# The first image's preparation reordered: its load on two queues, the weights' sums behind its parameters, four evictions moved to VectorE

## The chip, the cores and the metric

The kernel runs on one core of one Trainium2 chip. The metric is the device time of one execution in microseconds (us). Engines are named as in the profile: PE (TensorE; PEld is its weight load), DVE (VectorE), ACT (ScalarE), POOL (GpSimd) and SP (SyncE, which here only issues DMAs). ScalarE issues DMAs too; in the profile SP's DMA queue is q1 and ScalarE's is q10, and the issues themselves appear as SPq and ACTq.

## What is computed

The input x is 8 images of 256 channels, 56 by 56, fp32. Layer 0 is an involution on the group-normalised input: two 1x1 convolutions make a 7x7 kernel for each pixel and each of 16 channel groups, and this kernel weights the pixel's neighbourhood. Layer 1 is two 3x3 convolutions with ternary weights, each with a batch norm. Both layers add their input.

```python
def _L0_conv_ref(x, w_reduce, b_reduce, w_span, b_span):
    ker = jnp.einsum('bchw,oc->bohw', x, w_reduce) + b_reduce[None, :, None, None]
    ker = jnp.einsum('bchw,oc->bohw', ker, w_span) + b_span[None, :, None, None]
    ker = ker.reshape(B, G, 1, K * K, H, W)
    ...
    out = (ker * patches).sum(axis=3)
    return out.reshape(B, C, H, W)
...
# --- layer 0 (conv_preact) ---
x = x + _L0_conv_ref(_gn(x), L0_conv_w_reduce, ...)
# --- layer 1 (conv_preact) ---
x = x + _L1_conv_ref(_gn(x), L1_conv_w1, ...)
```

`_gn` normalises each image in 32 groups of 8 channels, without a scale or shift of its own. `_L1_conv_ref` quantizes each weight tensor to -1, 0, 1 by thresholds from its mean, maximum and minimum, and adds the centre tap once more.

## The kernel before, in words

The first phase is the involution. An image is cut into four quarters of 64 channels (`NCQ` = 4); a quarter's tile `x` holds 128 partitions (64 channels by two half images) of 1568 elements, and is loaded by `load_x` in two DMAs of 392 KB. Ahead of the loop over quarters and rows stands a preparation, and only there does the change edit anything. Each engine works through its own instructions in the order in which the program text issues them (a scheduler keeps that order here, and a helper `pin` fixes it inside the loop). The preparation runs as follows.

- **Loads.** ScalarE's queue issues five constants through `loaded` (L114: grp_sb, and g1, b1, g2, b2 of the two batch norms). SP's queue issues the eight pieces of the first image (L610). ScalarE then issues the constants made by `fixed` (L677: rims_sb, ident_sb, half_sb), br and wr in two pieces each (L693, L694), wl (L695) and bt (L696). SP issues the first 3x3 weights into `wf` in two pieces (L703), the span weights and their biases for the sums (L942, L943), and the first five neighbourhood tiles q (L728), two of which use the buffers of those two loads again.
- **Statistics.** VectorE takes bn_stats over each piece of x (L149) and aggregates them for each quarter (L620).
- **Sums.** VectorE sums the span weights over the 49 taps into `wsum` and `bsum` (L945) and spreads `wsum` into `wsx` (L946). `wsx` is the weight of the matmuls `ks` (L786), and `bsum` goes into `shift` (gn1b, L638), a bias of the same step; both are read at the end of the quarter's preparation.
- **Parameters.** `params(0)` averages the statistics over groups by a matmul with grp_sb (L156), copies the means out of PSUM (gm, L160), does a second matmul for the variance (L168), adds epsilon (ve, L135), takes the square root on ScalarE (L137), and refines its reciprocal on VectorE. It scales the reducing weights wr into `wrn` (L629), makes the scales `gn1s` (L636), `shift` (L638), and, through the matmuls br (L644), the bias `brn` (L647). The matmuls rim (L651) carry the means to the padding.
- **Reduction.** The first 1x1 convolution, matmuls pk (L713), is evicted by ScalarE into `kr` with the bias brn (L722). In between, a generator `extremes` searches wf: VectorE takes maximum and minimum of six pieces (L224, L225), ScalarE sums each piece (L227), and small matmuls (L255, L256, L265) combine them across partitions.
- **Generation.** `generate(0, 0, ...)` makes the per-pixel kernels of the first quarter: 14 units, each a pair of PSUM banks filled by matmuls pg (L820). Six banks are in rotation, so three units are in flight. ScalarE evicts the second bank (odd groups) with one activation for each position in the unit, and another for the last row's part where there is one (L824); VectorE evicts the first bank (even groups) with one or two additions (L828). The units take 3, 3 and 2 positions for each of two group pairs, and then 4 positions each. The matmuls ks and their activations (L794) end the quarter.

Then the loop over rows begins, with the matmuls pa (L852). In it the same generator works one quarter ahead. After the involution come the two 3x3 convolutions (matmuls L522) and a last elementwise pass. The compiled streams give each DMA one of eight completion semaphores in turn, in the order of the text, and a DMA's issue waits, on its own queue's engine, until the earlier DMA with the same semaphore has landed.

Of the kernel before, what the change touches and what calls it, by code (L numbers as in the profile page):

```python
# [11 lines left out]
ALU = mybir.AluOpType  # L12
AX = mybir.AxisListType
# [4 lines left out]
P = 128  # L18
# [3 lines left out]
K, PAD, G = 7, 3, 16  # L22
KK = K * K
# [5 lines left out]
CH = P // 2  # L29
NCQ = C // CH  # L30
GQ = G // NCQ
# [10 lines left out]
NQ = QY * QX  # L42
# [15 lines left out]
          32: (2, 0, 3), 33: (2, 3, 3), 34: (2, 6, 3)}  # L58
A_COLS = (NT * NP + NE * PX) * GQ

PER_ROW = (2, 2, 2, 1, 2, 2, 1, 2, 2, 0)
NQB = 5
PLEAD = 2
# [26 lines left out]
def involution_tri_block_kernel(  # L90
# [3 lines left out]
    nc = tc.nc  # L94
# [14 lines left out]
    def const_tile(shape, name):  # L109
        return const.tile(shape, F32, tag=name, name=name)  # L110

    def loaded(shape, name, src):
        t_ = const_tile(shape, name)
        nc.scalar.dma_start(t_, src)  # L114
        return t_

    grp_sb = loaded([P, P], "grp_sb", grp)
# [33 lines left out]
    def group_norm_params(mv, dst, psum_tile, name, means=None):  # L151


        n = mv.shape[1]
        ps = psum_tile(f"gnp_{name}")
        nc.tensor.matmul(ps[:, :2 * n], grp_sb, mv.rearrange("p n s -> p (n s)"),  # L156
                         start=True, stop=True)
        yield
        gm = small.tile([P, n, 2], F32, tag=f"gn_gm{n}", name=f"gm_{name}")
        nc.vector.tensor_copy(gm.rearrange("p n s -> p (n s)"), ps[:, :2 * n])  # L160
        if means is not None:
            means.append(gm)
        d = small.tile([P, n], F32, tag=f"gn_d{n}", name=f"d_{name}")
        nc.vector.tensor_tensor(d, mv[:, :, 0], gm[:, :, 0], ALU.subtract)
        nc.vector.tensor_tensor(d, d, d, ALU.mult)
        yield
        ps2 = psum_tile(f"gnp2_{name}")
        nc.tensor.matmul(ps2[:, :n], grp_sb, d, start=True, stop=True)  # L168
        yield
        var = small.tile([P, n], F32, tag=f"gn_var{n}", name=f"var_{name}")  # L170
        nc.vector.tensor_tensor(var, ps2[:, :n], gm[:, :, 1], ALU.add)
        rs = rstd_of(var, GN_EPS, name)
        nc.vector.tensor_copy(dst[:, :, 0], rs)
        nc.vector.scalar_tensor_tensor(dst[:, :, 1], gm[:, :, 0], -1.0, rs, ALU.mult, ALU.mult)
# [404 lines left out]
    with ExitStack() as ph1:  # L579
# [3 lines left out]
        def ps_bank(name):  # L583
            return ps_p.tile([P, 512], F32, tag="ps", name=name)

        def ps_pair(name):
            return [ps_bank(f"{name}_{i}") for i in range(2)]

        def ps_one(name):
            ps = row_ps[-1] if row_ps else ps_a.tile([P, 512], F32, tag="pa", name=name)  # L590
            return ps[:, TX * 2 * NP:]
# [10 lines left out]
        work = ph1.enter_context(tc.tile_pool(name="work", bufs=2))  # L602
        apool1 = ph1.enter_context(tc.tile_pool(name="apool1", bufs=1))

        def load_x(b, c, j):

            if j == 0:
                xs[b, c] = xpool.tile([P, NHW], F32, tag="x", name=f"x_{b}_{c}")
            part = slice(j * NHW // 2, (j + 1) * NHW // 2)
            nc.sync.dma_start(xs[b, c][:, part], x[b, c, :, part])  # L610

        def gn1_stats(b, c, j):

# [5 lines left out]
            if j == NCB - 1:  # L619
                nc.vector.bn_aggr(mvs[b][:, c, :], gst1[c].rearrange("p n s -> p (n s)"))  # L620

        def params(b):


            dst = small.tile([P, NCQ, 2], F32, tag="gn1", name=f"gn1_{b}")
            means = []
            yield from group_norm_params(mvs.pop(b), dst, ps_one, f"a{b}", means)
            for c in range(NCQ):
                nc.vector.tensor_scalar(  # L629
                    wrn[:, c, :].rearrange("p (i r) -> p i r", i=2),  # L630
                    wr[:, c, :].unsqueeze(1).to_broadcast([P, 2, CR]),
                    dst[:, c, 0:1], None, ALU.mult)

            scales = small.tile([P, NCQ, 2 + GQ], F32, tag="gn1s", name=f"gn1s_{b}")
            for c in range(NCQ):
                nc.vector.tensor_scalar(scales[:, c], half_sb, dst[:, c, 0:1], None, ALU.mult)  # L636
            shift = small.tile([P, NCQ], F32, tag="gn1b", name=f"gn1b_{b}")
            nc.vector.tensor_tensor(shift, dst[:, :, 1], bsum, ALU.mult)  # L638
            for _ in range(3):
                yield  # L640
            ps = ps_one(f"br_{b}")
            for c in range(NCQ):
                for i in range(2):
                    nc.tensor.matmul(ps[i * CR:(i + 1) * CR, :1], wr[:CH, c, :], dst[:CH, c, 1:2],  # L644
                                     start=(c == 0), stop=(c == NCQ - 1))
            yield
            nc.vector.tensor_tensor(brn, br, ps[:, :1], ALU.add)  # L647
            yield
            ps = ps_bank(f"rim_{b}")
            for c in range(NCQ):  # L650
                nc.tensor.matmul(ps[:NQ, c * P:(c + 1) * P],  # L651
                                 means[0][:, c, 0:1].to_broadcast([P, NQ]), ident_sb,
                                 start=True, stop=True)
            rim = small.tile([P, NCQ, P], F32, tag="rim", bufs=1, name=f"rim_{b}")
            nc.scalar.copy(rim[:NQ].rearrange("p c f -> p (c f)"), ps[:NQ, :NCQ * P])
            prm[b] = dst, scales, shift, rim
# [11 lines left out]
        gst1, mvs = {}, {}  # L668
        prm, xs = {}, {}
        for c in range(NCQ):  # L670
            for j in range(2):
                load_x(0, c, j)

        def fixed(shape, name, src=None, pool=fix):
            t_ = pool.tile(shape, F32, tag=name, name=name)
# [7 lines left out]
        bt = fixed([NQ, NCQ, GQ, NP], "bt", pool=early)  # L683

        wsum, wsx = fixed([P, G], "wsum"), fixed([P, NCQ, CH], "wsx")
        rims_sb = fixed([P, 5], "rims_sb", rims)
        bsum = fixed([P, NCQ], "bsum")
# [6 lines left out]
            nc.scalar.dma_start(wr[j * CH:(j + 1) * CH], w_red.rearrange("(t p) o -> p t o", p=CH))  # L694
        nc.scalar.dma_start(wl, w_line)  # L695
        nc.scalar.dma_start(bt, b_tile)  # L696


        nf = CT * 9 * C
# [100 lines left out]
                    nc.gpsimd.tensor_tensor(x_, x_, v, ALU.add)  # L800
                yield

        def generate(b, c, a):

            whole, rest = (v.rearrange("q t (g p) -> q g p t", g=GQ) for v in views(a))
            for u, (gp, p0, n) in enumerate(UNITS):
                ps = ps_pair(f"pg_{b}_{c}_{u}")
                nt = NT + (NE if p0 < PX else 0)  # L810
                g = 2 * gp
                parts = [(whole, 0, NT)] + ([(rest, NT, nt)] if NT < nt else [])

                for j in range(n):
                    py, px = (p0 + j) // PX, (p0 + j) % PX
                    o = py * QX + px
                    for i in range(2):
                        rows = slice(i * CR, (i + 1) * CR)
                        dst = ps[0][:NQ, j:n * nt:n] if i == 0 else ps[1][:NQ, j * nt:(j + 1) * nt]
                        nc.tensor.matmul(dst, wl[rows, c, gp, o:o + NQ], kr[py][rows, px, :],  # L820
                                         start=True, stop=True)
                for j in range(n):
                    for dst, t0, t1 in parts:
                        nc.scalar.activation(  # L824
                            dst[:, g + 1, p0 + j], ps[1][:NQ, j * nt + t0:j * nt + t1],
                            AF.Identity, bias=bt[:, c, g + 1, p0 + j:p0 + j + 1])
                for dst, t0, t1 in parts:
                    nc.vector.tensor_tensor(  # L828
                        dst[:, g, p0:p0 + n].rearrange("q p t -> q t p"),
                        ps[0][:NQ, t0 * n:t1 * n].rearrange("q (t p) -> q t p", p=n),  # L830
                        bt[:, c, g, p0:p0 + n].unsqueeze(1).to_broadcast([NQ, t1 - t0, n]), ALU.add)
                yield
            yield from constant(b, c)
# [37 lines left out]
        queue = [(b, c, ty) for b in range(B) for c in range(NCQ) for ty in range(TY)]  # L871
# [66 lines left out]
        for _ in range(2):  # L938
            held.append(qpool.tile([P, TX, P], F32, tag="q", name=f"sums{len(held)}"))
        wv, bv = (t_.rearrange("p k c -> p (k c)")[:, :n_ * KK]  # L940
                  for t_, n_ in zip(held, (G, NCQ)))
        nc.sync.dma_start(wv, w_all)  # L942
        nc.sync.dma_start(bv, b_all)  # L943
        for dst, v in ((wsum, wv), (bsum, bv)):
            nc.vector.tensor_reduce(dst, v.rearrange("p (g k) -> p g k", k=KK), AX.X, ALU.add)  # L945
        nc.vector.tensor_copy(wsx.rearrange("p c (g i) -> p (c g) i", g=GQ),  # L946
                              wsum.unsqueeze(2).to_broadcast([P, G, CH // GQ]))
        pin(start=True)
        for _ in params(0):
            pass  # L950
        a_next = matrices(0)
        thresholds = [pieces.tile([P, n], F32, tag=f"cols{n}", name=f"cols{n}") for n in (24, 42)]
# [9 lines left out]
        for _ in range(NQB):  # L962
            prefetch()
        surround(PLEAD)
        for u, _ in enumerate(generate(0, 0, a_next)):
            next(found, None)
            pin()
        for _ in found:
# [17 lines left out]
        for m, (b, c) in enumerate(quarters):  # L986
            a = a_next
            gen = iter(())
            if m + 1 < len(quarters):
                a_next = matrices(m + 1)  # L990
                gen = generate(*quarters[m + 1], a_next)
            more = b + 1 < B
            for ty in range(TY):
# [23 lines left out]
                next(norm, None)  # L1017
                for _ in range(PER_ROW[ty]):
                    next(gen, None)
# [59 lines left out]
    with ExitStack() as ph4:  # L1079
# [10 lines left out]
        for j in range(B * CT):  # L1090
            b, t = j // CT, j % CT
            y1f, y2f, x1f = (home(name, j) for name in ("y1", "y2", "x1"))
            n = {B * CT - 2: 2, B * CT - 1: 4}.get(j, 1)
# [96 lines left out]
```

## Time and profile before

| | before |
|---|---|
| median of three runs | 2163.53 us (2159.11 to 2166.13) |
| profiled execution | 2164.76 us, of which span 2163.0 us |
| mean granted PE clock | 0.911 |
| PE, DVE, ACT, POOL busy | 81%, 81%, 66%, 27% |
| first row's matmul (pa) begins | 61.89 us into the span |
| data read and written in HBM | 323.28 MB, 112.20 MB |

The profile is of one execution; times in the trace count from the start of its span. A line of the timeline has the start, the duration from the first of a merged group's start to its last's end, the engine with the source line, the operation, what it writes and reads, the number of instructions, and in brackets the idle time of the engine before it with what ended that. Matmuls and activations overlap with their successors, so that a group's duration divided by its count is the pace, and less than the mean of one. A line of the waits has the engine and line that waited, on whom, and the sum, number and longest of the waits in us.

### The profile page before, as it was taken

What the parts mean: (1) busy time and instruction counts of PE and PEld (TensorE: products, weight loads), DVE (VectorE), ACT (ScalarE), POOL (GpSimd) and SP (SyncE); (2) the same over time, 40 slices, a digit from 0 to 9 for tenths busy, and PEclk for the clock granted to TensorE, in tenths of its full rate; (3) what the DMA queues carried; (4) which work ended last, traced back from release to release, by engine and by line L of the source; (5) the groups of instructions that cost most, each with busy time, mean ns of one, the idle gap of its engine ahead of it and who ended that gap; (6) DMA issues with size and microseconds to landing.
All of it is one profiled execution on the core that took longest, in us unless ns stands there. A gap on an engine that the chain in (4) does not pass through costs nothing.

```text
span 2163.0 us, 70724 instructions
## 1 busy us (share of the span) xinstructions
PE 1759.3 (81%) x29680; PEld 1632.6 (75%) x29680; DVE 1753.4 (81%) x3337; ACT 1432.2 (66%) x3553; POOL 590.7 (27%) x965
## 2 busy tenths in 40 slices
PE   4988988989899898988699999997999999960000
PEld 4777777878777687777699999997999999960000
DVE  5777978787777868877699999998999999984444
ACT  3877787877767677777366666665566666653344
POOL 0555566555546646666200000000000000000000
PEclk9999999999989999999799999998999999985555
DMA  5667777686767758667733333335323333369999
GB/s 184 212 178 232 220 211 236 195 266 197 244 185 218 239 164 263 191 203 201 254 122 122 122 122 122 122 122 189 118 114 124 124 128 128 124 262 425 429 428 397
DMA packets 156250, 440.06 MB, mean 203 GB/s; under 512 B 63774, under 2 KB 74012, under 8 KB 148508
## 3 DMA queue, kind: packets, MB, share of 16 engines
q1 hardware_dynamic: 150336, 405.50, 55.2%
q10 hardware_dynamic: 5596, 30.03, 3.3%
q8 instruction: 235, 3.85, 0.8%
q14 instruction: 83, 0.68, 0.1%
HBM read 323.28 MB, written 112.20 MB: 201 GB/s over the span
## 4 chain that ended last, share of the span: by engine, by line
PE 68%; DMA 10%; DVE 9%; issue 6%; POOL 3%; ACT 3%; ACTq 0%; SPq 0%; POOLq 0%; DVEq 0%
PE c L522 40%; PE pg L820 14%; PE pa L852 8%; PE pk L713 3%; DMA y1f<-y1d 3%; DMA x1f<-x1d 2%; PE ks L786 2%; DMA out_y<-x1f 2%; POOL q L751 1%; DVE x1f L1102 1%; DVE inv L864 1%; ACT a L824 1%; DMA y2f<-y2d 1%; POOL x L868 1%; DMA q<-in_x_nb 1%
## 5 line engine op out<-in xcount | busy, mean ns | idle before, releaser
L522 PE MATMUL c<-pl,wq 128*128 128x392 f32 x4608 | 857.7, 348 | 14.9 <-ACT pl L392 14.9
L522 PEld LDWEIGHTS c<-pl,wq 128*128 128x128 f32 x4608 | 855.7, 190 | 16.7 <-ACT pl L392 15.3
L824 ACT ACTIVATE a<-pg,bt 126x126 f32<-126x126 f32 (+1 forms) x2048 | 530.1, 469 | 110.1 <-PE pg L820 109.5
L820 PE MATMUL pg<-kr,wl 64*126 64x140 f32 (+1 forms) x6144 | 466.1, 296 | 41.2 <-issue 16.4
L820 PEld LDWEIGHTS pg<-kr,wl 64*126 64x126 f32 x6144 | 405.5, 198 | 67.2 <-issue 24.3
L852 PE MATMUL pa<-a,q 126*32 126x48 f32 x17024 | 290.4, 215 | 67.0 <-issue 52.6
L852 PEld LDWEIGHTS pa<-a,q 126*32 126x32 f32 x17024 | 242.1, 116 | 135.4 <-issue 83.6
L828 DVE TENSOR_TENSOR a<-pg,bt 126x504 f32<-126x504 f32 (+4 forms) x640 | 280.9, 480 | 54.4 <-PE pg L820 52.8
L868 POOL TENSOR_TENSOR x<-x,inv 128x168 f32<-128x168 f32 x320 | 167.0, 522 | 404.1 <-DVE inv L864 370.7
L864 DVE SCALAR_TENSOR_TENSOR inv<-pa,gn1s,inv 128x168 f32<-128x168 f32 (+1 forms) x384 | 134.2, 351 | 154.6 <-ACT inv L862 151.1
L392 ACT CAST pl<-r 128x812 fp32r<-128x812 f32 x192 | 162.5, 868 | 143.4 <-DVE r L387 122.8
L372 POOL MEMSET xp<- 128x116 f32 x32 | 6.3, 196 | 826.1 <-DVE a L387 826.1
L751 POOL TENSOR_TENSOR q<-q,sides 126x256 f32<-126x256 f32 (+1 forms) x320 | 225.5, 705 | 3.1 <-DMA q<-in_x_nb 3.1
L393 DVE TENSOR_TENSOR pl<-r,pl 128x812 fp32r<-128x812 f32 x192 | 186.6, 998 | 27.6 <-ACT pl L392 26.3
L457 ACT ACTIVATE dummy<-y,nc 128x1568 f32<-128x1568 f32 (+1 forms) x128 | 200.2, 1564 | 4.8 <-DVE y L542 3.5
L862 ACT ACTIVATE inv<-pa,gn1s 128x168 f32<-128x168 f32 x320 | 134.9, 423 | 69.5 <-PE pa L852 49.3
L149 DVE BATCH_NORM_STATS2 st<-x 128x6 f32<-128x392 f32 x256 | 137.8, 554 | 16.4 <-DMA x<-in_x 10.1
L800 POOL TENSOR_TENSOR x<-x,add 128x504 f32<-128x504 f32 (+1 forms) x128 | 127.2, 1024 | 25.4 <-ACT add L794 25.4
L1049 ACT ACTIVATE xp<-raw,gn 128x392 f32<-128x392 f32 (+1 forms) x124 | 82.5, 721 | 61.3 <-DVE a L387 61.0
L1069 ACT ACTIVATE xp<-raw,bi_bn,sc_bn 128x392 f32<-128x392 f32 (+1 forms) x124 | 82.3, 720 | 58.8 <-DVE a L387 57.1
L1100 DVE SCALAR_TENSOR_TENSOR y1f<-y2f,sc_bn,y1f 128x3136 f32<-128x3136 f32 (+2 forms) x20 | 56.6, 2831 | 64.6 <-DMA y2f<-y2d 50.6
L713 PE MATMUL pk<-x,wrn 64*128 64x168 f32 (+1 forms) x1152 | 101.0, 316 | 0.0
(174 smaller groups left out, 1789.2 us busy)
## 6 DMA issues: line engine op xcount, KB each, us to landing
q<-in_x_nb SPq DMA_DIRECT2D x320, 448.0 KB, 4.2
raw<-x1d SPq DMA_DIRECT2D x32, 812.0 KB, 5.9
raw<-y1d SPq DMA_DIRECT2D x32, 812.0 KB, 6.1
x<-in_x SPq DMA_DIRECT2D x64, 392.0 KB, 5.3
x1d<-x SPq DMA_DIRECT2D x64, 392.0 KB, 5.2
y1d<-y SPq DMA_DIRECT2D x30, 784.0 KB, 3.7
y2d<-y SPq DMA_DIRECT2D x30, 784.0 KB, 3.4
y1f<-y1d SPq DMA_DIRECT2D x14, 1568.0 KB, 14.4
```

Source lines behind the costliest of these rows:

```text
L392: nc.scalar.copy(hi, r)
L393: nc.vector.tensor_tensor(lo, r, hi.bitcast(F32), ALU.subtract)
L457: nc.scalar.activation(dst, v, f, bias=shift[:, to:to + 1], accum_out=stats[:, to, j, n:n + 1])
L522: nc.tensor.matmul(ps[:, to, :NM], wq[k][:, t, dx, to * P:(to + 1) * P], part[:, t, :, dx:dx + W], start=(c == 0), stop=(c == last))
L713: nc.tensor.matmul(ps[h][:, :m * W], wrn[rows, c, :], src[rows, r0:r0 + (m - 1) * PY + 1:PY, :], start=(c == 0), stop=(c == NCQ - 1))
L751: nc.gpsimd.tensor_tensor(v, v, z, ALU.add)
L820: nc.tensor.matmul(dst, wl[rows, c, gp, o:o + NQ], kr[py][rows, px, :], start=True, stop=True)
L824: nc.scalar.activation(dst[:, g + 1, p0 + j], ps[1][:NQ, j * nt + t0:j * nt + t1], AF.Identity, bias=bt[:, c, g + 1, p0 + j:p0 + j + 1])
L828: nc.vector.tensor_tensor(dst[:, g, p0:p0 + n].rearrange("q p t -> q t p"), ps[0][:NQ, t0 * n:t1 * n].rearrange("q (t p) -> q t p", p=n), ...
L852: nc.tensor.matmul(ps[o:o + m, k * w:(k + 1) * w], q[:NQ, k, o:o + m], av[:, t + k, g * w:(g + 1) * w], start=True, stop=True)
L864: nc.vector.scalar_tensor_tensor(iv, parts[:, :, g], scale[:, g:g + 1], iv, ALU.mult, ALU.add)
L868: nc.gpsimd.tensor_tensor(xv, xv, iv.rearrange("p t (y x) -> p y t x", x=PX), ALU.add)
```

## The change

It has three parts, all ahead of the loop.

- The eight pieces of the first image are issued alternately by SP and ScalarE, ahead of every constant. The five constants of `loaded` are only noted in a list; grp_sb is issued by ScalarE right behind the image, and g1, b1, g2 and b2 behind bt.
- The sums of the span weights and biases, and `shift`, which needs one of them, are computed inside `params(0)` behind brn instead of ahead of it. Their loads stay where they are in SP's order.
- In `generate(0, 0, ...)`, and for this quarter alone, the second bank of units 1, 4, 7 and 10 is evicted by VectorE, by one addition for all positions of the unit (and another for the last row's part in units 1 and 4), instead of by ScalarE's activations.

```diff
+FIRST = (1, 4, 7, 10)
...
+    later = []
+
     def loaded(shape, name, src):
         t_ = const_tile(shape, name)
-        nc.scalar.dma_start(t_, src)
+        later.append((t_, src))
         return t_
...
-        def load_x(b, c, j):
+        def load_x(b, c, j, queue=nc.sync):
...
-            nc.sync.dma_start(xs[b, c][:, part], x[b, c, :, part])
+            queue.dma_start(xs[b, c][:, part], x[b, c, :, part])
...
-        def params(b):
+        def params(b, sums=None):
...
-            nc.vector.tensor_tensor(shift, dst[:, :, 1], bsum, ALU.mult)
+            if sums is None:
+                nc.vector.tensor_tensor(shift, dst[:, :, 1], bsum, ALU.mult)
...
             nc.vector.tensor_tensor(brn, br, ps[:, :1], ALU.add)
+            if sums is not None:
+                sums()
+                nc.vector.tensor_tensor(shift, dst[:, :, 1], bsum, ALU.mult)
...
         for c in range(NCQ):
-            for j in range(2):
-                load_x(0, c, j)
+            for j, queue in enumerate((nc.sync, nc.scalar)):
+                load_x(0, c, j, queue)
+        for t_, src in later[:1]:
+            nc.scalar.dma_start(t_, src)
...
         nc.scalar.dma_start(wl, w_line)
         nc.scalar.dma_start(bt, b_tile)
+        for t_, src in later[1:]:
+            nc.scalar.dma_start(t_, src)
...
-        def generate(b, c, a):
+        def generate(b, c, a, shared=()):
...
-                for j in range(n):
+                for j in range(0 if u in shared else n):
                     for dst, t0, t1 in parts:
                         nc.scalar.activation(
...
+                for dst, t0, t1 in parts if u in shared else ():
+                    nc.vector.tensor_tensor(
+                        dst[:, g + 1, p0:p0 + n],
+                        ps[1][:NQ, :n * nt].rearrange("q (p t) -> q p t", t=nt)[:, :, t0:t1],
+                        bt[:, c, g + 1, p0:p0 + n].unsqueeze(2).to_broadcast([NQ, n, t1 - t0]),
+                        ALU.add)
...
-        for dst, v in ((wsum, wv), (bsum, bv)):
-            nc.vector.tensor_reduce(dst, v.rearrange("p (g k) -> p g k", k=KK), AX.X, ALU.add)
-        nc.vector.tensor_copy(wsx.rearrange("p c (g i) -> p (c g) i", g=GQ),
-                              wsum.unsqueeze(2).to_broadcast([P, G, CH // GQ]))
+
+        def sums():
+            for dst, v in ((wsum, wv), (bsum, bv)):
+                nc.vector.tensor_reduce(dst, v.rearrange("p (g k) -> p g k", k=KK), AX.X, ALU.add)
+            nc.vector.tensor_copy(wsx.rearrange("p c (g i) -> p (c g) i", g=GQ),
+                                  wsum.unsqueeze(2).to_broadcast([P, G, CH // GQ]))
+
         pin(start=True)
-        for _ in params(0):
+        for _ in params(0, sums):
             pass
...
-        for u, _ in enumerate(generate(0, 0, a_next)):
+        for u, _ in enumerate(generate(0, 0, a_next, FIRST)):
```

## The prediction, made before the run

> **What bounds the kernel now.** I read the page's opening first, for how the engines share the span, then its chain of waits, then the stretch that the change touches, by time.
>
> ```profile
> span 2163.0 us, 70724 instructions
> PE 1759.3 (81%) x29680; PEld 1632.6 (75%) x29680; DVE 1753.4 (81%) x3337; ACT 1432.2 (66%) x3553; POOL 590.7 (27%) x965
> PE c L522 40%; PE pg L820 14%; PE pa L852 8%; PE pk L713 3%; DMA y1f<-y1d 3%; DMA x1f<-x1d 2%; PE ks L786 2%; DMA out_y<-x1f 2%; POOL q L751 1%; DVE x1f L1102 1%; DVE inv L864 1%; ACT a L824 1%; DMA y2f<-y2d 1%; POOL x L868 1%; DMA q<-in_x_nb 1%
> ```
>
> The reader sees a kernel carried by matmuls; what the change edits lies wholly ahead of the first row of the loop, whose matmul (pa, L852) starts at 61.89 us. So the stage, not the shares of the whole, decides. The busy time by stretch (us, PE, PEld, DVE, ACT, POOL, clock, DMA share, GB/s):
>
> ```profile
> 0.00:10.00 10.00, 0.00 (x0) 0.00 (x0) 3.42 (x8) 0.00 (x0) 0.20 (x4) 1.00 0.67 207
> 10.00:20.00 10.00, 0.59 (x2) 0.50 (x2) 5.63 (x13) 1.28 (x1) 0.00 (x0) 1.00 1.01 363
> 20.00:30.00 10.00, 1.40 (x18) 1.31 (x18) 4.10 (x20) 0.20 (x1) 0.00 (x0) 1.00 1.01 394
> 30.00:40.00 10.00, 10.00 (x88) 9.76 (x89) 10.00 (x17) 4.57 (x13) 4.27 (x8) 1.00 0.08 28
> 40.00:50.00 10.00, 8.81 (x124) 8.24 (x122) 4.34 (x21) 10.00 (x38) 0.00 (x0) 1.00 0.00 1
> 50.00:60.00 10.00, 9.46 (x148) 8.75 (x145) 7.26 (x20) 10.00 (x45) 0.00 (x0) 1.00 0.01 3
> ```
>
> For 30 us no engine works much and the DMA is full only from 10 us on. The timeline of VectorE and PE there shows two holes:
>
> ```profile
> 16.54 1.04 DVE L149 BATCH_NORM_STATS2 st<-x 128x6 f32<-128x392 f32 x2 [2.06 <-DMA x<-in_x]
> 17.93 1.04 DVE L149 BATCH_NORM_STATS2 st<-x 128x6 f32<-128x392 f32 x2 [0.35 <-DMA x<-in_x]
> 19.32 0.59 PE L156 MATMUL gnp_a<-mv,grp_sb 128*128 128x8 f32 x2 [19.32 <-DVE mv L620]
> 24.67 0.97 DVE L945 TENSOR_REDUCE wsum<-sums 128x16 f32<-128x784 f32 x1 [5.41 <-DMA sums<-in_w_all]
> 26.02 0.16 DVE L160 COPY gm_a<-gnp_a 128x8 f32<-128x8 f32 x1
> 27.66 0.20 ACT L137 ACTIVATE sq_a<-ve_a 128x4 f32<-128x4 f32 x1 [14.36 <-DVE ve_a L135]
> 32.13 12.90 PE L713 MATMUL pk<-x,wrn 64*128 64x168 f32 x144
> ```
>
> First, the image is complete only at 17.9 us. Second, the group means are in PSUM by 19.9, but VectorE, in order, stands at the sums' reduce until their DMA lands at 24.67. Then the parameters take 26.02 to 32.13. Why the image is late, the waits of SP's own queue tell:
>
> ```profile
> SPq L610 <- DMA b_sb<-in_b: 4.4, 1, 4.4
> SPq L610 <- DMA x<-in_x: 2.0, 1, 2.0
> ```
>
> The fourth piece of x waited 4.4 us for a 1 KB constant: the compiled streams use eight completion semaphores round robin, so each DMA waits, on its issuing engine, for the landing of the one eight before it.
>
> [...] So a wait ahead of a DMA issue on ScalarE holds the activations behind it; the trace agrees (bt issued at 11.40 for 0.59, table load at 12.01). [...] 394 GB/s from SP nearly alone (20 to 30). [...] wl on ScalarE's queue took 97.2% of the DMA engines from 13 to 14 us while x pieces of SP waited.
>
> **The change part by part.**
>
> *1, x on two queues ahead of the constants.* Nothing is added: the same 8 pieces of 392 KB (3.21 MB) and the same constants, reordered. Issues need 4 x 0.45 = 1.8 us on each queue and no longer wait for a semaphore. Before, 3.0 us had passed when the DMA ran at full rate; I take 0.3 MB by then, and 2.9 MB at 400 GB/s after it: data complete at 10.3. Landing shows about 1.0 later (x pieces: last packets near 16.7, stats at 17.93): **11.3 instead of 17.9**. The last stats (1.04) and aggregate (0.26) end at 12.7. VectorE's whole stats work, 16 x 0.52 + 4 x 0.2 = 9.1 us from about 4, ends at 13.1 or so too. If the constant grp_sb is there (it queues behind x on ScalarE's queue, and may have to let the first half of wf pass), the matmul L156 starts at 13, else at 14.5; ve is ready 1.9 later, **at 15 to 16.5**.
>
> *2, sums behind brn.* VectorE loses the wait of 5.41 and 1.35 us of reduces and copy ahead of gm. They come back behind brn, with their DMA long landed (about 21, since sums_b waits on the landing of wf's second half). Queued behind them are the 12 reduces of wf (L224, L225), begun 1.6 us later relative to pk; who waits for these is ScalarE's accumulation L227, which took its last piece at 45.91 when the reduces had ended at 40.97. That slack of 4.9 hides 1.6; without it the cost would be 1.6. POOL (idle until 32.91) and SP's q loads (two reuse the sums' buffers, issued at 25.67 before, some 1.5 us earlier now, needed from row 3) don't notice.
>
> *3, the new order on ScalarE's queue: what is late next.* After the four x pieces ScalarE issues grp, rims, ident, half, br, wr, br, wr, wl, bt and then g1, b1, g2, b2, and only then its table load and the square root. Counting the semaphores round: the first half of wf follows x; the second wr waits for it; the last b2 waits for that wr. So: wf's first half (1.18 MB, 2.9 us) goes out behind x and the small constants: data to 13.5, landed at 14.5. The wr is issued then. Its landing took 5.4 before (beside other transfers), ident 2.5 (nearly alone); I take 4.0: 18.5. Then b2's issue 0.49 and the table load 1.28 (before: 12.01, hidden; now on the path): the square root starts at **20.3**. VectorE's ve has waited since 16.5 at latest. wrn needs that same wr, so it is late in any case. Ends: 18.8 (landing 2.5) and 22.7 (wf a microsecond later, 5.4).
>
> From the square root to pk nothing changes: 27.66 to 32.13 before, 4.47 us (VectorE chain, br, rim). **Gain 27.66 - 20.3 = 7.4 us**, ends 8.9 and 5.0.
>
> *4, VectorE evicts the odd half of units 1, 4, 7, 10.* ScalarE loses 6 + 6 + 4 + 4 = 20 of its 64 activations; 64 took 15.24 us, so 4.8. VectorE gains four evictions of the sizes that it has: 378 + 42 elements at 0.61 together, twice, and 504 at 0.68, twice: 2.6 us.
>
> ```profile
> 46.73 15.24 ACT L824 ACTIVATE a<-pg,bt 126x126 f32<-126x126 f32 x64
> 47.64 0.38 PE L255 MATMUL ends_w<-cols,piece_w 128*128 128x1 f32 x2 [1.18 <-DVE piece_w L249]
> 51.71 8.39 PE L820 MATMUL pg<-kr,wl 64*126 64x126 f32 x128 [0.54 <-DVE a L828]
> 60.03 1.93 PE L786 MATMUL ks<-kr,wsx 64*64 64x504 f32 x16
> ```
>
> [...] ScalarE looks full, but PE does not stand for it: 128 matmuls in 8.39 us are 65.5 ns each, the pace of the 32 ahead (2.18/32 = 68). ScalarE is one unit behind at the end, which holds the second pair of ks banks and so costs some 0.6. Against that, unit 1's extra 0.61 stands ahead of VectorE's read of ends_w, on whose result PE waits in order (all_w, L265): units 6 and on come 0.5 later. **Net 0**, ends 0.7 gain and 0.7 loss.
>
> *Sum.* 7.4 + 0 against the profiled execution's 2164.76 (span 2163.0 and 1.8 around it) is 2157.4. The median of the runs is 1.2 lower, so 2156.1; I say 2156. Behind the first row both programs have the same instructions in the same order, each released by others and none by the hour, so the head start stays.
>
> **Rivals.** (a) *The square root is not held by ScalarE's queue* (constants slip through between transfers; wr lands as soon as ve is ready). Then ve decides: 27.66 - 16.5 to 15 is 11.2 to 12.7 gain, less the wait for wr: about 2152.5. For it: small constants landed in 2.1 to 2.5 at 5 to 8 us. Against: b2's place in line. (b) *The gain is half lost*: two queues load x no faster beside wf, or wr stands behind both halves of wf (9.9 to 10.8 us to landing before). With wf landing at 16 and wr 7 later the square root starts at 24.8, gain 2.9, and with VectorE's 0.7 of part 4 lost, 2161. (c) *Slower: the chain x, wf, wr, b2, table load becomes longer than the old wait.* Its place is ScalarE's last issue; it decides from a square root at 27.7 on. With wf's first half landing 10.3 after the end of x (21.6) and wr another 10.3 (31.9), the square root is at 33.7, 6 late, with 0.7 of part 4 2170. Against: SP has only x ahead of that half. (d) The change may not do what it says only in that x arrives no sooner because bandwidth bounds; but 67% DMA share in the first 10 us leaves room.
>
> **How the numbers follow.** The likeliest case has 0.68, (a) 0.13, (b) 0.13, (c) 0.06. About 0.3%, 6.5 us, is what a measurement of this kernel can tell from no change: faster means under 2157.0. The likeliest value passes that by 1 us only; with its ends and the spread of the runs (2159.11 to 2166.13) I give it 0.51 faster and 0.17 same. (a) adds 0.13 faster, (b) 0.12 same and 0.01 slower, (c) 0.06 slower: 0.64, 0.29, 0.07. Range: 2150.5 takes in (a), 2161 takes in (b); (c) is left out.
>
> **What would show it.** Right: the last stats near 12 to 13, L156 at 13 to 14.5, a square root that waits for ScalarE's issues and starts at 19 to 22 with the table load directly ahead, pk 4.5 later, first row near 54.5, and pg still at 66 ns. Wrong: a square root released by ve (a); wr landing after 20 (b); pk after 32 (c); or a first row whose lead over before is not that of pk, which would put part 4 or the sums on the path.

## The result and the profile after

| | before | after |
|---|---|---|
| median, runs side by side on one chip | 2162.17 us (2153.31 to 2166.83, 11 runs) | 2154.21 us (2151.54 to 2166.93, 11 runs) |
| profiled execution | 2164.76 us, span 2163.0 | 2152.45 us, span 2150.7 |
| square root of the first parameters | 27.66 us | 19.39 us |
| first matmul of the reduction (pk) | 32.13 us | 23.88 us |
| first row's matmul (pa) | 61.89 us | 53.95 us |

The ratio of the runs, after to before, is 0.9975 with a 95% interval of 0.9957 to 0.9992: about 5.4 us faster, between 1.7 and 9.3. The difference of the medians is 7.96 us, the lead at the first row 7.94 us. Single executions of one kernel differ by more than 10 us, so below I compare the start of the first row, and use the timed ratios as a bound only.

The opening of the page after:

```profile
span 2150.7 us, 70705 instructions
PE 1751.9 (81%) x29680; PEld 1624.7 (76%) x29680; DVE 1757.3 (82%) x3343; ACT 1430.8 (67%) x3533; POOL 590.7 (27%) x965
```

The shares of the whole tell nothing, as before. By stretch of 10 us (start:end, length, then PE, PEld, DVE, ACT, POOL, clock, DMA share, GB/s):

```profile
0.00:10.00 10.00, 0.00 (x0) 0.00 (x0) 5.14 (x13) 0.00 (x0) 0.20 (x4) 1.00 0.83 312
10.00:20.00 10.00, 1.15 (x4) 1.00 (x4) 4.32 (x15) 1.49 (x2) 0.00 (x0) 1.00 0.86 301
20.00:30.00 10.00, 9.07 (x84) 8.84 (x86) 8.55 (x24) 3.41 (x10) 4.11 (x8) 1.00 0.93 314
```

The first 10 us move 312 GB/s where before had 207, and the third stretch, with 1.40 us of PE before, has 9.07 now. The timeline of PE, ScalarE and VectorE says how (line numbers are those of the changed kernel: L160 was L156, L141 was L137, L725 was L713, L965 was L945):

```profile
14.50 0.56 PE L160 MATMUL gnp_a<-mv,grp_sb 128*128 128x8 f32 x2 [14.50 <-DMA grp_sb<-in_grp]
16.54 0.17 DVE L139 TENSOR_SCALAR ve_a<-var_a 128x4 f32<-128x4 f32 x1
17.61 0.46 ACTq L708 DMA_DIRECT2D b_sb<-in_b  x1
18.09 1.28 ACT L141 ACT_TABLE_LOAD   x1 [18.09 <-issue]
19.39 0.20 ACT L141 ACTIVATE sq_a<-ve_a 128x4 f32<-128x4 f32 x1
22.79 0.97 DVE L965 TENSOR_REDUCE wsum<-sums 128x16 f32<-128x784 f32 x1 [0.48 <-DMA sums<-in_w_all]
23.88 12.32 PE L725 MATMUL pk<-x,wrn 64*128 64x168 f32 x144
```

The statistics are complete at 13.2 us (the last aggregate is at 12.93 for 0.27), but the group matmul stands until its constant grp_sb has landed. VectorE has ve at 16.71. The square root starts 2.7 us later, and no idle time stands before it: ScalarE issued DMAs without a pause from 13.97 to 18.07 and then loaded its table. The sums are now behind all this, and wait only 0.48 us for their data. How far instructions overlap, their means tell: the 144 matmuls pk in 12.32 us are 85.6 ns apart, where one takes 332 or 349 ns by its form; before's 64 activations of pg in 15.24 us are 238 ns apart, where one takes 778 or 443.

### The profile page after: what moved, and what is told of

The parts are those of the page before. It is cut to its first block, busy times and chain, and to the rows that moved or that the text cites. A ratio compares the mean times of both kernels' runs of the same rounds, so it can differ in the third digit from the quotient of the medians.

```text
span 2150.7 us, 70705 instructions
## 1 busy us (share of the span) xinstructions
PE 1751.9 (81%) x29680; PEld 1624.7 (76%) x29680; DVE 1757.3 (82%) x3343; ACT 1430.8 (67%) x3533; POOL 590.7 (27%) x965
## 4 chain that ended last, share of the span: by engine, by line
PE 67%; DVE 10%; DMA 10%; issue 6%; ACT 4%; POOL 4%; ACTq 0%; SPq 0%; POOLq 0%; DVEq 0%
PE c L526 40%; PE pg L832 14%; PE pa L870 7%; PE pk L725 4%; DMA y1f<-y1d 3%; DMA x1f<-x1d 2%; ACT a L836 2%; POOL q L763 2%; DMA out_y<-x1f 2%; PE ks L798 1%; DVE x1f L1123 1%; DVE inv L882 1%; POOL x L886 1%; DVE a L846 1%; DMA y2f<-y2d 1%
## 5 line engine op out<-in xcount | busy, mean ns | idle before, releaser
L526 PEld LDWEIGHTS c<-pl,wq 128*128 128x128 f32 x4608 | 854.8, 189 | 16.7 <-ACT pl L396 15.3
L836 ACT ACTIVATE a<-pg,bt 126x126 f32<-126x126 f32 x2028 | 526.2, 455 | 118.4 <-PE pg L832 117.4
L832 PE MATMUL pg<-kr,wl 64*126 64x140 f32 (+1 forms) x6144 | 460.5, 294 | 45.3 <-issue 16.2
L832 PEld LDWEIGHTS pg<-kr,wl 64*126 64x126 f32 x6144 | 399.4, 196 | 68.0 <-issue 23.8
L846 DVE TENSOR_TENSOR a<-pg,bt 126x504 f32<-126x504 f32 (+4 forms) x640 | 280.4, 480 | 40.4 <-PE pg L832 38.8
L725 PE MATMUL pk<-x,wrn 64*128 64x168 f32 (+1 forms) x1152 | 101.1, 315 | 0.6 <-issue 0.6
```

The source lines that it names most:

```text
L526: nc.tensor.matmul(ps[:, to, :NM], wq[k][:, t, dx, to * P:(to + 1) * P], part[:, t, :, dx:dx + W], start=(c == 0), stop=(c == last))
L725: nc.tensor.matmul(ps[h][:, :m * W], wrn[rows, c, :], src[rows, r0:r0 + (m - 1) * PY + 1:PY, :], start=(c == 0), stop=(c == NCQ - 1))
L836: nc.scalar.activation(dst[:, g + 1, p0 + j], ps[1][:NQ, j * nt + t0:j * nt + t1], AF.Identity, bias=bt[:, c, g + 1, p0 + j:p0 + j + 1])
L846: nc.vector.tensor_tensor(dst[:, g, p0:p0 + n].rearrange("q p t -> q t p"), ps[0][:NQ, t0 * n:t1 * n].rearrange("q (t p) -> q t p", p=n), ...
```

## The experiments

Two stretches make up most of the way from pk to the first row, and I read them apart, for a reason that the clock records gave. **Pace of pk.** From pk to pg took 11.32 to 12.84 us in the 14 profiles, by no part of the change: two executions of one kernel (e6, below) have both ends. The windows of the matmuls pk and their activations alone, of one microsecond each (PE, PEld and ACT, then clock, DMA share, GB/s), count them; first e6, then e6 again:

```profile
22.35:23.35 1.00, 1.00 (x10) 1.00 (x10) 0.00 (x0) 1.00 1.04 362
24.35:25.35 1.00, 1.00 (x10) 1.00 (x10) 0.34 (x2) 1.00 1.02 401
28.35:29.35 1.00, 1.00 (x20) 1.00 (x17) 0.30 (x3) 1.00 0.26 94
```

```profile
22.51:23.51 1.00, 1.00 (x16) 1.00 (x16) 0.00 (x0) 1.00 1.00 342
23.51:24.51 1.00, 1.00 (x18) 1.00 (x18) 0.70 (x2) 1.00 1.04 402
```

Ten a microsecond still in the fourth in one (20 later), 16 in the second and 18 in the third in the other. The trace's records of the granted clock begin 4.32 us after the start of pk in the first and 1.22 us after it in the second (the column shows 1.00 ahead of that too, where there is no record). In all 14 profiles, pk to pg less half of that slow stretch is 10.68 to 10.71 us. So PE starts pk at half pace, for a time (the slow stretch) that differs from one execution to the next. The last column below takes it out.

| kernel | square root | pk | slow stretch | pg to ks | first row | first row less half the slow stretch |
|---|---|---|---|---|---|---|
| before | 27.66 | 32.13 | 4.11 | 15.16 | 61.89 | 59.83 |
| after | 19.39 | 23.88 | 2.92 | 16.06 | 53.95 | 52.49 |
| e10, after again | 19.65 | 24.14 | 4.31 | 15.77 | 54.61 | 52.45 |
| e1, sums alone | 20.98 | 25.46 | 1.68 | 15.16 | 54.03 | 53.19 |
| e2, loads alone | 26.61 | 31.08 | 2.03 | 15.17 | 59.83 | 58.82 |
| e3, without evictions | 19.47 | 23.95 | 4.08 | 15.11 | 53.64 | 51.60 |
| e5, evictions alone | 27.72 | 32.20 | 3.32 | 16.00 | 62.41 | 60.75 |
| e4, g and b late | 17.48 | 21.95 | 4.11 | 15.78 | 52.33 | 50.28 |
| e6, table early | 16.87 | 21.35 | 4.32 | 15.11 | 51.16 | 49.00 |
| e6 again | 17.04 | 21.51 | 1.22 | 15.13 | 49.82 | 49.21 |
| e7, needed first | 19.16 | 23.64 | 2.02 | 15.11 | 52.32 | 51.31 |
| e9, wr ahead | 19.42 | 23.91 | 4.14 | 15.11 | 53.63 | 51.56 |
| e8, not unit 1 | 23.26 | 27.74 | 3.31 | 15.22 | 57.17 | 55.52 |
| e11, not unit 1 again | 19.75 | 24.25 | 2.67 | 15.30 | 53.44 | 52.10 |

**Which part carries the gain: each alone, and without the third.** e1 is the kernel before with the sums moved behind brn and nothing else; e2 has the new order of loads alone; e3 is the change without its evictions.

```diff
 e1, to before:
-        (reduces of wsum, bsum and the copy wsx ahead of params)
-        for _ in params(0):
+        for _ in params(0, sums):
 e3, to after:
-        for u, _ in enumerate(generate(0, 0, a_next, FIRST)):
+        for u, _ in enumerate(generate(0, 0, a_next)):
 e2, to e3: the sums ahead of params(0) again
```

> The kernel before with part 2 alone: the sums behind brn; x stays on SP's queue behind the five constants, ScalarE evicts every unit. Theory A (the wait for the sums' DMA was the link that held the parameters; the image's later arrival comes next): gm follows the group matmul at about 19.95 instead of 26.02, the square root at 21.6, pk at 26.0 to 26.3 (6 earlier than before's 32.13), first row at about 55.9, so some 6 us less in all, three quarters of the whole change. Theory B (the earlier image brought most of it): pk moves by less than 2 us, since the sums' DMA only moves its wait to behind brn, where pk's eviction needs VectorE; then the whole change's 8.25 come from the two queues.

> The kernel after with the sums put back ahead of the parameters and no eviction moved: part 1 alone. Theory A: the image and its statistics are done at about 13.2 as in after, but VectorE then stands at the sums' reduce until their DMA lands at 23 to 24.6 (sums_b waits for the second half of wf), gm at about 25.4, square root at 27, pk at 31 to 32: within 1 us of before, a time within 2 us of before. Theory B: the earlier image carries the gain, pk at 24 to 26, and some 6 to 8 us less in all.

> The kernel after without part 4: ScalarE evicts all units of the first quarter. Theory A (part 4 is worth nothing net): pk at 23.9 as in after and from pk to the first row 29.8 us as in before (29.76) against 30.07 in after, so first row at 53.6 to 54.0 and the same total within the spread. Theory C (part 4 gains 0.6 or more, which a lower PE clock from 40 to 50 us, 0.83, hid in after's profile): first row at 54.4 or later, if the clock is 1.0 there; at 0.83, 55 or later.

e1, timeline of ScalarE and PE:

```profile
20.98 0.20 ACT L137 ACTIVATE sq_a<-ve_a 128x4 f32<-128x4 f32 x1 [7.18 <-DVE ve_a L135]
25.46 11.71 PE L717 MATMUL pk<-x,wrn 64*128 64x168 f32 x144
```

e2, timeline of VectorE and ScalarE:

```profile
23.06 0.97 DVE L963 TENSOR_REDUCE wsum<-sums 128x16 f32<-128x784 f32 x1 [9.85 <-DMA sums<-in_w_all]
26.61 0.20 ACT L141 ACTIVATE sq_a<-ve_a 128x4 f32<-128x4 f32 x1 [6.96 <-DVE ve_a L139]
```

Timed, e1 has the ratio 0.9977 (0.9964 to 0.999), e2 1.0007 (0.9988 to 1.0027), e3 0.9976 (0.9963 to 0.999). In e1 the square root waits for ve alone, and pk is 6.67 us earlier than before. In e2 VectorE, with the image there early, stands 9.85 us at the sums instead of 5.41: the wait took up the whole gain but 1.05 us at pk. Both together (e3) bring 8.18. The early image is worth 1.5 us once the sums are out of the way, and 1.05 without that.

**What holds the square root.** e4 takes the four loads g1, b1, g2, b2 from ScalarE's queue and lets SP issue them behind the first rows' q; e6 does that too, leaves the evictions out, and has ScalarE do a square root of a constant behind its x pieces, so that the table is loaded there.

```diff
 e4, to after:
-        for t_, src in later[1:]:
-            nc.scalar.dma_start(t_, src)
...
         surround(PLEAD)
+        for t_, src in later[1:]:
+            nc.sync.dma_start(t_, src)
 e6, to e4: generate(0, 0, a_next), and ahead of grp_sb's load
+        warm = const_tile([P, 1], "warm")
+        nc.gpsimd.memset(warm, 1.0)
+        nc.scalar.activation(warm, warm, AF.Sqrt)
```

> The kernel after with the loads of g1, b1, g2 and b2 issued by SP behind the first five q loads instead of by ScalarE ahead of its table load. Theory A (ScalarE's queue holds the square root: in after ve is ready at 16.71 and the root begins at 19.39): four issues of about 0.5 us less, the table load at about 16.0 to 16.1 instead of 18.09, the square root at 17.4, pk 1.9 to 2.0 earlier at about 21.9, if wr has landed by then (17.0 to 17.8) and the scaled weights wait for nothing new; first row at about 52.0, and 2 us less in all. Rival D (the second wr, landing at 17 to 17.8, or the sums behind brn set the pace): pk moves by less than 1 us.

> The kernel with g1, b1, g2, b2 on SP behind the first q loads as before this run, no eviction moved, and one more activation: a square root of one constant column right behind ScalarE's four x issues, where ScalarE waits for a landing anyway, so that the table load stands there. Theory A: the square root of the parameters no longer waits for ScalarE, it starts as ve is ready, 16.8 (17.48 with the four loads moved alone), and pk at 21.3, if the second wr lands by 18.1; first row at 50 to 51. Rival D (wr's landing is next): pk between 21.4 and 22, the br matmuls released by the DMA of wr and not by gn.

> The kernel of the early table load (g1, b1, g2, b2 behind the first q loads on SP, one square root of a constant column behind ScalarE's x issues, no eviction moved), timed. Its first row stood at 51.16, 10.7 earlier than before's and 2.8 earlier than after's. If the head start stays as it did for after: 10 to 11 us less than before in all, a ratio of about 0.995; square root at 16.9 and pk at 21.4 again unless a wr lands late; full clock from pg to ks and 15.1 there under theory F, half clock with some chance under rival G.

e4, timeline of ScalarE:

```profile
16.18 1.28 ACT L141 ACT_TABLE_LOAD   x1 [16.18 <-DMA br<-in_b_red]
17.48 0.20 ACT L141 ACTIVATE sq_a<-ve_a 128x4 f32<-128x4 f32 x1
```

e6, second execution, the same view:

```profile
2.83 1.28 ACT L683 ACT_TABLE_LOAD   x1 [2.83 <-issue]
17.04 0.21 ACT L141 ACTIVATE sq_a<-ve_a 128x4 f32<-128x4 f32 x1 [12.70 <-DVE ve_a L139]
```

Four issues less ahead of the table load brought pk 1.93 us forward. With the table loaded at 2.83, ScalarE waits for ve, and pk is another 0.4 to 0.6 earlier. e4's ratio is 0.9964 (0.9946 to 0.9981), with the evictions in it. e6's is **0.9926 (0.99 to 0.9952)**, median 2148.5 us of 6 runs beside 2164.77 us of before: this version beats both kernels, the change by 3.2 to 3.5 us at the first row (last column). Of these, 2.4 to 2.6 are left against e3, which has no evictions either; the rest is the evictions left out.

**Can the small loads go ahead of the image?** e7 gives ScalarE grp_sb and both wr first and SP the whole image; e9 has grp_sb and wr ahead of ScalarE's half of the image. The rest is as in e6.

```diff
 e9, to e6: order of issue on ScalarE
-        x (four pieces), warm, grp_sb, rims, ident, half, br, wr, br, wr, wl, bt
+        grp_sb, wr, wr, x (four pieces), warm, br, br, ident, half, rims, wl, bt
 e7, to e6: SP issues all eight x pieces, ScalarE
+        grp_sb, wr, wr, warm, br, br, ident, half, rims, wl, bt
```

> The kernel with the loads ordered by need: ScalarE issues grp and wr first, then the square root of one constant column (the table load), then br, ident, half, rims, wl, bt; SP issues all eight x pieces, wf, the sums, the first q loads, then g1, b1, g2, b2; sums behind brn as in after, no eviction moved. Theory A (the image's bandwidth and its statistics are the last bound): the image complete at 11.5 to 12, last aggregate at about 13.2, the group matmul right behind it and not at 14.5, square root at 15.3, pk at 19.8, first row at 48.4 to 49.5, 12 to 13.5 us earlier than before, and about 12 us less in all. Rival E (x on one queue is slower, as it waits again for a semaphore: the sixth to eighth pieces need grp and wr landed): a hole in the DMA ahead of the fifth piece, last aggregate at 15 or later, pk at 21.5 or later.

> The kernel of the early table load with grp and both wr pieces issued by ScalarE ahead of its four x pieces, and br, ident, half, rims behind them. Theory A (grp's landing at 14.6 and wr's at 18.4 are what holds the parameters in the early-table kernel): the image complete some 0.5 to 1 later than there, last aggregate at about 13.5 to 14.2, the group matmul right behind it, square root at 15.6 to 16.3, pk at 20.1 to 20.8, first row at 49.3 to 50.5, about 12 us less than before in all. Rival E (as with x on one queue, the last x pieces wait for landings and share the DMA with wf and wl): last aggregate at 15.5 or later and pk no earlier than 21.4.

e7, timeline of VectorE:

```profile
15.49 1.04 DVE L153 BATCH_NORM_STATS2 st<-x 128x6 f32<-128x392 f32 x2 [2.00 <-DMA x<-in_x]
```

Both lose more at the image than they win at the constants. The last aggregate ends at 16.83 in e7 and 17.09 in e9, against 13.2 in after, because the last pieces of x are issued later (at 9.17 in e7, where SP's eight issues take from 0.74 to 9.50, and at 5.73 in e9, against 2.15 in after) and come in beside what else has been issued by then (wl at 8.98 in e7, wf at 6.06 in e9), with the DMA's share at 1.03 in both from 10 to 20 us (387 and 405 GB/s). e7: pk 23.64, ratio 0.9954 (0.9937 to 0.9971). e9: pk 23.91, ratio 0.9955 (0.994 to 0.9971). Their pk is 2.1 to 2.6 us behind e6's; the intervals of the ratios overlap with e6's.

**What the evictions cost.** e5 adds them alone to the kernel before. e8 and e11 are the change with units 4, 7 and 10 only; e10 is the change once more.

```diff
 e5, to before: the branch on `shared` in generate, and generate(0, 0, a_next, FIRST)
 e8 and e11, to after:
-FIRST = (1, 4, 7, 10)
+FIRST = (4, 7, 10)
```

> The kernel before with part 4 alone. From the first pg matmul to the first ks matmul the runs without part 4 took 15.16 (before), 15.16, 15.17 and 15.11 us, those with it 16.06 (after) and 15.78. Theory C1 (part 4 itself costs that: unit 1's extra eviction keeps PE waiting at all_w, and the PE clock drops to 0.5 to 0.6 for some 3 us right after that idle stretch): 15.7 to 16.1 here too, with granted clock under 0.8 in the 4 us behind all_w, pk at 32.1, first row at 62.3 to 62.8, later than before's 61.89. Rival C2 (the drop belongs to the earlier start, not to part 4): 15.2 or less and clock 1.0.

> The kernel after with VectorE evicting units 4, 7 and 10 but not unit 1. Theory C1: VectorE reads ends_w 0.7 to 0.8 earlier, PE waits at all_w no longer than in before (0.2), no drop of the clock, and from pg to ks 15.1 us or a little less (down to 14.6, if ScalarE's lag at the end of the generation was worth the half microsecond that it was given), first row at 53.0 from pk at 23.9. Rival C3 (VectorE's slower evictions, 0.8 to 1.04 us each, hold PE's banks later in the generation): still 15.6 or more at clock 1.0.

> The kernel after once more, for two things that one profile can't tell. First, the clock: all four profiles with part 4 show PE at half clock for about 3.4 us behind the first pg matmuls, none of the six without. Theory F (part 4 brings it on in every execution): again half clock for some 3.4 us, and 15.8 to 16.1 from pg to ks. Rival G ([...] part 4 at most makes it likelier): full clock this time, and then pg to ks shows what part 4 is worth at full clock, 14.5 to 15.1. Second, the second wr: landed by 17.6 the square root starts at 19.4; landing late as in the run without unit 1 (7.2 us after its issue) it starts at 23.3.

> The kernel after with VectorE evicting units 4, 7 and 10 but not unit 1, once more. It differs from the kernel without part 4 only behind the point where the clock had dropped in its first run. Rival G: full clock this time with a chance of a half or more, and then 14.3 to 15.0 from pg to ks instead of 15.22; theory F: half clock again and 15.2.

In the table's column from pg to ks, the eight profiles without evictions lie between 15.11 and 15.17 us. The four with all of them have 15.77 to 16.06, so they lose 0.6 to 0.95 us. The last column agrees: e5 against before is 0.92 later, after and e10 against e3 0.89 and 0.85 (of e10's, 0.18 is its later square root). The timed runs are too coarse for this: after and e3 have the ratios 0.9975 and 0.9976. The groups of VectorE in after, from pg to the first row, by form (busy and mean ns, idle before):

```profile
L846 DVE TENSOR_TENSOR a<-pg,bt 126x504 f32<-126x504 f32 x8 | 4.9, 665 | 0.0
L840 DVE TENSOR_TENSOR a<-pg,bt 126x504 f32<-126x504 f32 x2 | 2.1, 1045 | 0.3 <-PE pg L832 0.2
L840 DVE TENSOR_TENSOR a<-pg,bt 126x378 f32<-126x378 f32 x2 | 1.6, 790 | 0.8 <-PE pg L832 0.8
```

L840 is the added eviction, L846 the old one: the same operation and number of elements, 1045 ns against 665. And the clock fell. Windows cut every 3.41 us, the length of the shortest records of the granted clock, from the end of the slow stretch, the fourth and the fifth, of after:

```profile
37.04:40.45 3.41, 1.78 (x21) 1.21 (x19) 2.81 (x15) 2.71 (x11) 0.00 (x0) 1.00 0.01 2
40.45:43.87 3.42, 3.30 (x27) 3.29 (x29) 2.53 (x15) 1.85 (x10) 0.00 (x0) 0.50 0.02 5
```

of e3:

```profile
38.27:41.68 3.41, 2.24 (x26) 1.88 (x28) 2.63 (x16) 3.41 (x18) 0.00 (x0) 1.00 0.00 0
41.68:45.09 3.41, 2.87 (x48) 2.68 (x46) 2.93 (x14) 3.41 (x19) 0.00 (x0) 1.00 0.02 5
```

and of e8:

```profile
41.29:44.70 3.41, 2.22 (x28) 1.64 (x26) 2.62 (x16) 3.41 (x17) 0.00 (x0) 1.00 0.01 2
44.70:48.11 3.41, 3.41 (x36) 3.41 (x34) 3.00 (x14) 2.37 (x11) 0.00 (x0) 0.50 0.02 5
```

All six profiles with evictions, e8 and e11 among them, have the clock at 0.50 for one window of 3.41 us, the fifth after the slow stretch; PE does 27 to 36 matmuls in it, where the others do 41 to 48. The other eight have full clock for 18 windows or more. Six of six against none of eight looks like a proof, but the order of events in e8 and e11 speaks against it. Their clock falls at 44.70 and 40.57 us, and their first moved eviction, unit 4's, begins only 2.3 and 2.9 us later; in e8:

```profile
46.98 0.87 DVE L840 TENSOR_TENSOR a<-pg,bt 126x378 f32<-126x378 f32 x2 [0.20 <-PE pg L832]
```

Up to the fall, their matmuls pg start within 0.02 us of those of e1 and e3, counted from the first pg. So in these two the moved evictions did not set the drop off. What separates the six from the eight is how many matmuls begin in the window ahead of it, the fourth (the counts in the lines above also hold matmuls begun earlier): 14 to 22 against 25 to 28. The same shows elsewhere. In the first 300 us of the 14 profiles, fewer than 25 begin in 21 of the 1012 windows at full clock, these six among them, and a window at half clock follows each of the 21. The other 53 falls of that time come after windows with more matmuls, so the count is not the whole of it.

Two things lower the count. With unit 1's eviction PE stands longer ahead of all_w (0.57 us in after), and 14 to 19 begin. In e8 and e11, where 22 begin, what I take for the cause is where the window lies: their slow stretches, 3.31 and 2.67 us, lie between 2.03 and 4.08, where none of the eight profiles without evictions lies. after and e5 (2.92 and 3.32) lie there too, and might have fallen without evictions, which no run shows; e10 and e4 (4.31 and 4.11) lie beside before and e3 and fell, with 19 and 18. So there I put the drop, which before and e3 did not have, down to unit 1's eviction, while part of what after and e5 lost may be the place of the window. That the clock follows the number of matmuls is argued from these counts; **no run varied it alone**. Without unit 1, e8 and e11 are within 0.2 us of the kernels without evictions from pg to ks, drop included.

e8 showed something else by chance. Its order of loads is after's, and yet its square root came at 23.26. Its timeline of ScalarE:

```profile
21.60 0.34 ACTq L708 DMA_DIRECT2D b_sb<-in_b  x1
21.96 1.28 ACT L141 ACT_TABLE_LOAD   x1 [21.96 <-DMA sums<-in_w_all]
```

The first line is b2 (the bracket of the second names another load that landed at the same moment). The issue before it ended at 17.87. The second wr had been issued at 14.38 and landed at 21.58, 7.2 us later, and b2 went out right behind that landing. In after, wr landed 3.0 us after its issue, and b2 did not wait for it. In the six profiles with this order (after, e2, e3, e8, e10, e11) the table load came at 18.09 to 18.46 five times and at 21.96 once.

## Why the prediction was right, and where it was not

The forecast was 2156.0 us, a gain of 7.4; the median is 2154.21, and the lead at the first row, freed of the slow stretch, is 59.83 - 52.49 = 7.34 us. That it agrees so closely is luck: two errors of opposite sign, 0.9 us each, cancel.

- **The image and the statistics** (step 1): last stats and aggregate at 12.7 to 13.1, measured 13.2. Right, though a landing shows 0.7 us behind the last packets (near 17.2 in before, not 16.7) where the sum had 1.0. The new order brought earlier issues, and no more bandwidth that shows: all eight pieces were issued by 2.79 us, where SP alone had needed until 10.61, and the two queues moved 401 GB/s from 3 to 4 us, half each, where SP's alone moved 394 from 20 to 30 us in before. Of the two values for the group matmul, 13 and 14.5, the later came, at 14.50. grp_sb, issued at 5.07 behind x, took 9.3 us to land: the last x piece ahead of it on its queue landed at 11.59, and the first half of wf, beside it, at 13.95. ve was ready at 16.71, against 16.5 at latest.
- **The sums** (step 2): right, and larger than all else: e1 brings 6.67 of the 8.25 us at pk. Their reduces behind brn cost nothing that shows: e1 and e3 have 15.16 and 15.11 us from pg to ks, as before has, and pk to pg agrees in all profiles once the slow stretch is out.
- **What is late next** (step 3): right in its place, ScalarE's queue ahead of the table load; the size was off by 0.9, square root at 19.39 for 20.3, well within its ends. The mis-sized term is the wait of b2 for the second wr. I had wr issued at 14.5 and 4.0 us to its landing; it was issued at 13.97, behind the landing of wf's first half at 13.95, and landed at 16.94, before b2's turn came at 17.61. The semaphores were counted rightly: in after's trace wf's first half, that wr and b2 carry one number. Their turns go by the order in which the compiled program mixes the two queues' issues, not by that of the text: before's fourth piece of x has the number of b1, and was issued at 6.50, behind b1's landing at 6.48. Six issues (that wr, wl, bt, g1, b1, g2) of 0.47 to 0.67 us each fill the time between. The issues themselves were the limit, which the sum had only after the landing. e4 confirms it from the other side (four issues less, 1.93 us). e8 shows that the wait is no fiction: when wr lands late, b2 waits, for 3.7 us there.
- **From the square root to pk** I carried over 4.47 us; all profiles have 4.47 to 4.50.
- **The evictions** (step 4): wrong. "Net 0, ends 0.7 gain and 0.7 loss" was a loss of 0.9 in after and of 0.6 to 0.95 in the four profiles. The terms that failed are VectorE's new evictions, an estimate of 2.6 us from the old rows, measured as 0.83 + 0.90 + 1.04 + 1.05 = 3.8, and the clock at half for 3.41 us, which the sum did not have. PE's delay at all_w was right (0.57 us, for 0.5). ScalarE did lose its 20 activations, but it was not what PE waited for, as the prediction said.
- **The sum.** 8.25 at pk and 0.9 lost behind it make 7.35, where I had 7.4 and 0.

**The rivals.** (a), ve decides, did not come: the square root started 2.7 us after ve. It is what e6 makes happen. (b), a late wr, is not the usual course, but is what e8 met: its first row, at 57.17, keeps 4.7 us of the lead. (c), slower, did not come: even e8's square root is 4.4 us ahead of the old one. (d) falls with e1 and e2: the image does arrive early, and by itself that is worth 1.0 us.

How two queues share the DMA engines is shown for single stretches only, without harm to the sum. In before, from 13 to 14 us, 78 rows of wl, of 5152 bytes each, go out on ScalarE's queue for 6 rows of x on SP's. In after, from 12 to 13 us, it is 46 packets of SP's queue, rows of 9216 bytes, and 46 of ScalarE's, rows of 512 bytes: there a small load beside a large one got half of the packets, and 0.02 of the 0.45 MB. What sets the share of each queue stays open.

That the whole lead stays to the end is borne out only as far as the runs resolve: 7.3 us would be a ratio of 0.9966, inside the interval, and so are those of e1, e2, e4, e6, e7 and e9 by their own last column; e3's, 0.9962, is just outside its own.

## What to carry to other kernels

Ahead of a loop, first take away what stands in order before the critical work on an engine (here a reduce that waited for a DMA); faster loads alone are swallowed by it, 1.05 us of gain at pk instead of 8.2 with both. Then count what the DMA issues on an activation's queue cost that engine (0.47 to 0.67 us each for the six here), and move the issues that nobody needs yet, and the table load (1.28 us), to where the engine is idle anyway. Price an added operation by a row that reads and writes in the same order, not only one of the same size (1045 ns here, where the row of the same size had 665).

## What was not expected of the hardware

- **PE's granted clock changes in steps of 3.41 us.** Every record of it in the 14 profiles, but each one's last, which the end cuts short, lasts 3.41 us or a multiple, with 0.50 or 1.00. pk starts slow for 1.22 to 4.32 us, so that one program's first row can move by about 1.5 us from one execution to the next (1.34 between the two of e6). A comparison of milestones has to take that out first.
- **The same addition took VectorE 0.38 us more in another order.** L840 and L846 both add a bias to 504 elements of PSUM, in 1045 against 665 ns. L846 writes along the unit's positions, which are neighbours in the tile (the view `q t (g p)`); L840 writes along t, whose elements lie apart. The bias differs too: L840 repeats one value along its innermost run, L846 takes a new one at each element. Which of the two is the cause is not shown; no run changed either alone.
- **A small load's landing is uncertain.** The second wr, at the same place in the same order, landed 2.5 to 3.1 us after its issue in five profiles and 7.2 us in the sixth, e8. What delayed it there is open.
